# Bias sums ahead of the weights' product, transposed weights copied by ScalarE, u inside the product, and eight row tiles of layer 1 prepared during layer 0

## The chip, the cores and the metric

The kernel runs on one core of a Trainium2 chip. The metric is the device time of one execution in microseconds, as the median of several runs. The four runs of the kernel before agree within 0.32%. Ratios are the mean time of one kernel's runs over that of the other's from the same rounds, so they are not quite the ratio of the medians that stand beside them.

## The reference, cut to what matters

Two layers on 4096 nodes of 512 features. `adj` is a dense 4096 x 4096 matrix of 64 MB that both layers need.

```python
# layer 0: attention inside graphs of 128 nodes, adj as bias
h = relu(layernorm(x))
q = h @ Wq.T + bq;  k = h @ Wk.T + bk;  v = h @ Wv.T + bv
scores = (where(same_graph, q @ k.T * scale, 0) + adj + adj) * where(same_graph, 1, -1e6)
x = x + (softmax(scores) * same_graph) @ v
# layer 1: graph attention, 8 heads of 64
h  = relu(layernorm(x))
mx = einsum('nf,hfd->hnd', h, W)
t  = einsum('hnd,hd->hn', mx, a_dst)
x  = x + softmax(where(adj > 0, s_i + t_j, -inf)) @ mx      # s_i cancels in the softmax
```

## The kernel before

It has four stages. **Start (fold):** the product of Wq and Wk is formed once (`m_sb`), with the terms that the biases give (`c_sb`, `u_sb`, `z_sb`), so that layer 0 needs one projection for q and k together. **Layer 0's loop:** 16 groups `g` of two row tiles of 128 rows. Each group reads two rows of adj ahead (VectorE makes mask bytes, ScalarE sums exponentials, the bytes go out to DRAM), and does scores, values and attention. **Preparation of layer 1:** for each of 32 row tiles, a norm, four transposes, a projection (16 matmul instructions) and a weighting give a tile `part`. **Aggregation:** 3072 matmuls of masks with the parts.

```python
def fold(sb, tmp, work, ps_t, ps_p):
    wkT_sb = load_weight(...); wqT_sb = load_weight(...)
    for n, wT in enumerate((wkT_sb, wqT_sb)):
        ...
        for k in range(KC):                      # KC = 4
            pt = ps_t.tile([P, KC, P], F32, name="pt")        # 3 buffers in PSUM
            for m in range(KC):
                nc.tensor.transpose(pt[:, m, :], wT[:, k, ts(m, P)], ident)
            dst = w[:, :, ts(k, P)]
            if k % 2: nc.vector.tensor_copy(dst, pt)
            else:     nc.scalar.copy(dst, pt)
    for m in range(KC):                          # the product: 32 instructions
        ... matmul(pp, wq[:, k, ts(m, P)], wk[:, k, :]) ...
        nc.scalar.mul(m_sb[:, m, :], pp, SCALE)
    for b in (bk_sb, bq_sb):                     # a bias spread over all rows
        ... matmul(pp[:, ts(k, P)], b[:, k:k+1].to_broadcast([P, P]), ident) ...
    for dst, wT, row in ((u_col, wqT_sb, rows[0]), (c_sb, wkT_sb, rows[1])):
        ... nc.vector.scalar_tensor_tensor(wb, wT[:, k, :], SCALE, row, ..., accum_out=dst[:, k:k+1])
    ...                                          # u_sb and z_sb by matmul and ScalarE copy

for g in range(NG):                              # NG = 16 groups of layer 0
    ...
    s = scores(g, hT, gT, r, *look)
    prepare_on(); prepare_on()                   # only in the last group
    if not last: ngT = queries(nhT)
    sT = turned(s)                               # transposes of s, then a ScalarE copy
    for t in range(G):
        look_on(t)                               # reads adj for the next group
        attend(sT, vs[t], g, t)
        prepare_on()                             # only in the last group
        if not last: nvs.append(values(nhT, t))
    ...
for i in range(len(ahead) - 1, NT):              # the rest of layer 1's row tiles
    nhT = normed1(i + 1)
    prepare(i, hT, part_tile(...))
```

`prepare_on` norms and transposes the next row tile of layer 1 and projects the one before it. The order in the program is a wish, not the order on the chip: when the kernel is compiled, a scheduler moves instructions ahead of others.

## Time and profile before

| | |
|---|---|
| median of 4 runs | 983.44 us (982.24 to 985.37) |
| span of the profiled run | 981.0 us |
| TensorE busy | 947.1 us, 97% |
| mean granted TensorE clock | 0.986 |
| aggregation, not touched by the change | 489.0 us |

TensorE is nearly always busy, so a change of order can win only what it idles and what it loses while its granted clock is below 1 (0.89 on average in the start, 0.94 in the handover). The lines that show where this is stand in the prediction. A line of the timeline gives start, length, engine, source line, operation, and in brackets the idle time of the engine before it with what ended it; a line of the waits gives who waited for whom, the sum in us, the number of times and the longest.

### The profile page before, as it was taken

What the parts mean: (1) busy time and instruction counts of PE and PEld (TensorE: products, weight loads), DVE (VectorE), ACT (ScalarE), POOL (GpSimd) and SP (SyncE); (2) the same over time, 40 slices, a digit from 0 to 9 for tenths busy, and PEclk for the clock granted to TensorE, in tenths of its full rate; (3) what the DMA queues carried; (4) which work ended last, traced back from release to release, by engine and by line L of the source; (5) the groups of instructions that cost most, each with busy time, mean ns of one, the idle gap of its engine ahead of it and who ended that gap; (6) DMA issues with size and microseconds to landing.
All of it is one profiled execution on the core that took longest, in us unless ns stands there. A gap on an engine that the chain in (4) does not pass through costs nothing.

```text
span 981.0 us, 13168 instructions
## 1 busy us (share of the span) xinstructions
PE 947.1 (97%) x5051; PEld 820.8 (84%) x5051; DVE 461.6 (47%) x982; ACT 261.6 (27%) x501; POOL 180.3 (18%) x344
## 2 busy tenths in 40 slices
PE   6899999999999998999999999999999999999995
PEld 4477666766776676888899999999999999999995
DVE  3756866776675287655232423324233242342421
ACT  3676666676671222333100000000000000000000
POOL 1111211221121055555201101011010110101100
PEclk9899999999999998999999999999999999999998
DMA  9949898998992142222013133131221312312111
GB/s 347 419 181 370 352 370 333 377 367 346 368 371 77 59 129 80 65 65 70 6 43 87 50 81 83 47 86 50 80 85 45 86 51 80 86 44 86 50 38 36
DMA packets 58043, 148.28 MB, mean 151 GB/s; under 512 B 6387, under 2 KB 23027, under 8 KB 49779
## 3 DMA queue, kind: packets, MB, share of 16 engines
q1 hardware_dynamic: 48178, 130.31, 38.2%
q10 hardware_dynamic: 9792, 17.05, 4.6%
q8 instruction: 41, 0.67, 0.3%
q14 instruction: 32, 0.25, 0.1%
HBM read 113.77 MB, written 33.55 MB: 150 GB/s over the span
## 4 chain that ended last, share of the span: by engine, by line
PE 86%; DMA 4%; DVE 4%; ACT 3%; POOL 1%; issue 1%; SPq 0%; ACTq 0%; DVEq 0%
PE pg L284 50%; PE pp L418 10%; PE pp L244 9%; PE pp L406 8%; PE pp L491 3%; DMA a<-adj 3%; PE pss L464 2%; PE pt L127 2%; PE pp L190 2%; ACT junk L441 1%; DMA xg<-x 1%; ACT gT L410 1%; POOL part L232 1%; DVE row L121 1%; POOL rstd L120 0%
## 5 line engine op out<-in xcount | busy, mean ns | idle before, releaser
L284 PE MATMUL pg<-part,at 128*128 128x348 f32 x3072 | 489.0, 321 | 1.2 <-DVE e L253 1.2
L284 PEld LDWEIGHTS pg<-part,at 128*128 128x128 f32 x3072 | 488.7, 188 | 1.6 <-issue 1.6
L278 DVE CAST at<-at 128x4096 fp32r<-128x4096 fp8e4 x32 | 73.6, 2301 | 311.6 <-PE pg L284 311.6
L291 ACT COPY tot<-pg 128x522 f32<-128x522 f32 x32 | 19.1, 598 | 469.9 <-PE pg L284 469.9
L441 ACT ACTIVATE junk<-a 128x2048 bf16<-128x2048 f32 (+15 forms) x92 | 124.6, 1355 | 37.4 <-DMA a<-adj 19.4
L244 PE MATMUL pp<-w1x,hT 128*128 128x256 f32 (+1 forms) x512 | 119.5, 387 | 0.0
L418 PE MATMUL pp<-wv,hT 128*128 128x512 f32 x256 | 116.8, 599 | 1.0 <-ACT hT L128 1.0
L406 PE MATMUL pp<-hT,m_sb 128*128 128x256 f32 x512 | 113.2, 379 | 0.0
L244 PEld LDWEIGHTS pp<-w1x,hT 128*128 128x128 f32 x512 | 96.5, 193 | 14.3 <-issue 0.5
L406 PEld LDWEIGHTS pp<-hT,m_sb 128*128 128x128 f32 x512 | 96.1, 190 | 12.9 <-issue 0.5
L418 PEld LDWEIGHTS pp<-wv,hT 128*128 128x128 f32 x256 | 49.1, 193 | 62.0 <-issue 60.4
L136 DVE TENSOR_SCALAR a<-a 128x512 fp8e4<-128x512 f32 x256 | 94.6, 453 | 7.3 <-DMA a<-adj 4.7
L593 POOL COPY den_all<-tot 128x1 f32<-128x1 f32 x31 | 5.8, 186 | 368.2 <-DVE tot L292 368.2
L128 ACT ACTIVATE hT<-pt 128x512 f32<-128x512 f32 x64 | 37.7, 599 | 82.3 <-PE pt L127 82.3
L602 POOL TENSOR_TENSOR tot<-tot,row 128x512 f32<-128x512 f32 x31 | 40.0, 1289 | 62.0 <-DVE tot L297 62.0
L118 POOL TENSOR_SCALAR ve<-mv 128x1 f32<-128x1 f32 x64 | 16.2, 255 | 178.6 <-DVE mv L116 164.8
L232 POOL TENSOR_TENSOR part<-e,part 128x522 fp32r<-128x522 f32 x32 | 42.0, 1312 | 31.4 <-ACT part L231 27.8
L422 DVE TENSOR_TENSOR v<-pp,bv_sb 128x512 f32<-128x512 f32 x32 | 22.1, 691 | 42.3 <-PE pp L418 42.3
L271 DVE STREAM_TRANSPOSE at<-mw 128x1024 f32<-128x1024 f32 x32 | 39.6, 1238 | 0.0
L253 DVE TENSOR_TENSOR e<-pp,e 128x256 f32<-128x256 f32 x64 | 26.7, 418 | 25.3 <-ACT e L372 22.8
L410 ACT ACTIVATE gT<-pp,c_sb 128x256 f32<-128x256 f32 x64 | 29.9, 469 | 31.5 <-PE pp L406 31.4
L120 POOL TENSOR_TENSOR rstd<-ve,neghalf 128x1 f32<-128x1 f32 x64 | 36.8, 578 | 4.6
(94 smaller groups left out, 594.7 us busy)
## 6 DMA issues: line engine op xcount, KB each, us to landing
a<-adj SPq DMA_DIRECT2D x64, 1024.0 KB, 11.9
a_d<-a SPq DMA_DIRECT2D x32, 512.0 KB, 10.2
row<-x_d SPq DMA_DIRECT2D x64, 256.0 KB, 3.4
mw<-a_d SPq DMA_DIRECT2D x128, 128.0 KB, 4.0
xg<-x SPq DMA_DIRECT2D x16, 512.0 KB, 4.6
x_d<-x ACTq DMA_DIRECT2D x32, 256.0 KB, 4.3
out<-tot ACTq DMA_DIRECT2D x31, 256.0 KB, 3.8
wkT_sb<-wkT SPq DMA_DIRECT2D x4, 256.0 KB, 4.6
```

The source lines that it names most:

```text
L128: nc.scalar.activation(dst, pt, AF.Relu)
L136: nc.vector.tensor_scalar(a8v[:, u], av[:, u], 0.0, None, ALU.is_gt, saturate=False)
L232: nc.gpsimd.tensor_sub(dst[:, :, 1, :], e3, dst[:, :, 0, :].bitcast(F32))
L244: nc.tensor.matmul(pm[g][:, :n], hT[:, k, :], w1x[:, k, g * HW : g * HW + n], start=(k == 0), stop=(k == KC - 1),)
L271: nc.vector.transpose(at8.rearrange("p c n b -> p (c n b)").bitcast(F32).rearrange("p (c u n) -> p c u n", c=NW, n=B), mw.rearrange("p u ( ...
L278: nc.vector.tensor_copy(at.rearrange("p (c b) q -> p c b q", b=BY), at8.rearrange("p c q b -> p c b q"))
L284: nc.tensor.matmul(pg[:, c, : 2 * CW1], at[:, j, :], part(j)[:, c].rearrange("p s w -> p (s w)"), start=(j == 0), stop=(j == NT - 1),)
L406: nc.tensor.matmul(pp[:, : G * P], m_sb[:, k, ts(m, P)], hT[:, k, :], start=(k == 0), stop=(k == KC - 1),)
L410: nc.scalar.activation(gT[:, m, :], pp[:, : G * P], AF.Identity, bias=c_sb[:, m : m + 1])
L418: nc.tensor.matmul(pp, hT[:, k, ts(t, P)], wv[:, k, :], start=(k == 0), stop=(k == KC - 1))
L441: nc.scalar.activation(junk[:, c0:c1], a[:, c0:c1], AF.Exp, scale=2.0 * NEG, accum_out=sums[:, n : n + 1],)
L602: nc.gpsimd.tensor_add(num, num, row)
```

## The change

Its intent has two halves. The start is to lose its waits: the bias sums go into the gap in which TensorE waits for weights, all copies of transposed weights (PSUM to SBUF, 128 x 512) go to ScalarE, which takes 587 ns for one in the kernel before where VectorE takes 687 ns, u and z are formed in the middle of the product, and `hu` (each row of h times u, summed) comes after both norms. And eight row tiles of layer 1 are finished during layer 0: one `prepare_on` in every odd group from 3 on, and two more in the last.

```diff
         wkT_sb = load_weight(tmp, wkT, "wkT_sb", KC, tag="lo")
         wqT_sb = load_weight(tmp, wqT, "wqT_sb", KC, tag="lo")
+        def spread_bias(b):
+            pp = ps_p.tile([P, D], F32, name="pp")
+            for k in range(KC):
+                nc.tensor.matmul(
+                    pp[:, ts(k, P)], b[:, k : k + 1].to_broadcast([P, P]), ident,
+                    start=True, stop=True,
+                )
+            row = work.tile([P, D], F32, name="b_row", tag="hn")
+            nc.scalar.copy(row, pp)
+            return row
... (in the loop over the transposed pieces)
-                dst = w[:, :, ts(k, P)]
-                if k % 2:
-                    nc.vector.tensor_copy(dst, pt)
-                else:
-                    nc.scalar.copy(dst, pt)
+                nc.scalar.copy(w[:, :, ts(k, P)], pt)
+                if n == 0 and k == 0:
+                    rows = [spread_bias(b) for b in (bk_sb, bq_sb)]
... (the product and the bias sums are taken out here; the VectorE sums stay, and then)
+        for m in range(KC):
+            if m == 2:
+                ... (u_sb and z_sb, as before but here)
+            ... (the product, as before)
... (in normed)
+                    hns = []
                     for t in range(G):
                         hn = sb.tile([P, D], F32, name="hn")
                         norm(xg[g][:, t, :], hn)
                         relu_T(ps_t, hn, hT[:, :, ts(t, P)])
+                        hns.append(hn)
+                    for t, hn in enumerate(hns):
                         hu = sb.tile([P, D], BF16, name="hu", bufs=1)
... (in the loop over the groups)
-                    if g == 2:
+                    if g == 1:
                         w1x = load_w1(pool1, sb)
...
-                    def prepare_on():
-                        if last:
+                    def prepare_on(now):
+                        if now:
...
                     s = scores(g, hT, gT, r, *look)
-                    prepare_on()
-                    prepare_on()
+                    prepare_on(last)
                     if not last:
                         ngT = queries(nhT)
                     sT = turned(s)
+                    prepare_on(3 <= g and g % 2)
                     nvs = []
                     for t in range(G):
                         look_on(t)
                         attend(sT, vs[t], g, t)
-                        prepare_on()
+                        prepare_on(last and t == 0)
```

More of the change, by code (lines that the diff above doesn't have):

```diff
@@ L186, in fold @@
         z_sb = sb.tile([P, 1], F32, name="z_sb")
-        for m in range(KC):
-            pp = ps_p.tile([P, D], F32, name="pp")
-            for k in range(KC):
-                nc.tensor.matmul(
-                    pp, wq[:, k, ts(m, P)], wk[:, k, :], start=(k == 0), stop=(k == KC - 1)
-                )
-            nc.scalar.mul(m_sb[:, m, :], pp, SCALE)
-        rows = []
-        for n, b in enumerate((bk_sb, bq_sb)):
-            pp = ps_p.tile([P, D], F32, name="pp")
-            for k in range(KC):
-                nc.tensor.matmul(
-                    pp[:, ts(k, P)], b[:, k : k + 1].to_broadcast([P, P]), ident,
-                    start=True, stop=True,
-                )
-            row = work.tile([P, D], F32, name=f"b_row{n}", tag="hn")
-            nc.scalar.copy(row, pp)
-            rows.append(row)
         for dst, wT, row in ((u_col, wqT_sb, rows[0]), (c_sb, wkT_sb, rows[1])):
@@ L215, in fold @@
         )
-        pp = ps_p.tile([P, D], F32, name="pp")
-        for k in range(KC):
-            nc.tensor.matmul(
-                pp[:, ts(k, P)], u_col[:, k : k + 1].to_broadcast([P, P]), ident,
-                start=True, stop=True,
-            )
-        nc.scalar.copy(u_sb, pp)
-        pp = ps_p.tile([P, D], F32, name="pp")
-        nc.tensor.matmul(pp[:, :1], zp.to_broadcast([P, P]), one, start=True, stop=True)
-        nc.scalar.copy(z_sb, pp[:, :1])
+        for m in range(KC):
+            if m == 2:
+                pp = ps_p.tile([P, D], F32, name="pp")
+                for k in range(KC):
+                    nc.tensor.matmul(
+                        pp[:, ts(k, P)], u_col[:, k : k + 1].to_broadcast([P, P]), ident,
+                        start=True, stop=True,
+                    )
+                nc.scalar.copy(u_sb, pp)
+                pp = ps_p.tile([P, D], F32, name="pp")
+                nc.tensor.matmul(pp[:, :1], zp.to_broadcast([P, P]), one, start=True, stop=True)
+                nc.scalar.copy(z_sb, pp[:, :1])
+            pp = ps_p.tile([P, D], F32, name="pp")
+            for k in range(KC):
+                nc.tensor.matmul(
+                    pp, wq[:, k, ts(m, P)], wk[:, k, :], start=(k == 0), stop=(k == KC - 1)
+                )
+            nc.scalar.mul(m_sb[:, m, :], pp, SCALE)
         return m_sb, c_sb, u_sb, z_sb
```

## The prediction

> **What bounds the kernel now.** I read the busy shares of the page first, then the span cut into its stages, then the waits of TensorE stage by stage, then the timeline around each wait. In the busy line, PE is TensorE's matmuls and x is the number of instructions:
>
> ```profile
> PE 947.1 (97%) x5051; PEld 820.8 (84%) x5051; DVE 461.6 (47%) x982; ACT 261.6 (27%) x501; POOL 180.3 (18%) x344
> ```
>
> TensorE is the bound nearly everywhere, and the chain of work that ended last is 86% PE. The change adds and removes no matmul: it only reorders them. So it can gain at most TensorE's 981.0 - 947.1 = 33.9 us of idle time, plus what TensorE loses by running at a lower clock. The busy time by stage says where this is. I chose the borders from the timeline: end of the first `values`, end of the last group's first `scores` (layer 0's main loop), return to a steady pace, first aggregation matmul, last one. Columns: stretch, its length, busy us of each engine, granted clock, DMA share, GB/s:
>
> ```profile
> 0.00:48.38 48.38, 37.11 (x115) 21.16 (x116) 27.09 (x74) 25.50 (x39) 7.67 (x27) 0.89 0.98 382
> 48.38:342.10 293.72, 288.93 (x1227) 199.13 (x1227) 193.36 (x520) 174.29 (x330) 52.21 (x103) 1.00 0.77 299
> 342.10:397.12 55.02, 49.78 (x229) 40.74 (x228) 42.45 (x90) 15.24 (x37) 27.49 (x51) 0.94 0.36 99
> 397.12:480.30 83.18, 81.99 (x414) 70.94 (x412) 44.87 (x104) 26.85 (x63) 46.01 (x100) 1.00 0.21 58
> 480.30:969.33 489.03, 489.00 (x3072) 488.70 (x3072) 150.94 (x185) 19.14 (x32) 46.96 (x63) 1.00 0.23 64
> 969.33:981.00 11.67, 0.30 (x1) 0.08 (x1) 2.93 (x11) 0.60 (x1) 0.00 (x0) 0.58 0.10 32
> ```
>
> The first number after each length is PE. Idle: 11.3 us in the start (at a mean clock of 0.89), 4.8 in layer 0's loop, 5.2 in the handover from layer 0 to layer 1's preparation (at 0.94), 1.2 before the aggregation, nothing in the aggregation, 11.4 in the tail. The last two stages, half of the span, are not touched. What TensorE waited for in the start, in the loop and in the handover (three answers of the waits; us, times, longest):
>
> ```profile
> PE pt L174 <- DMA wkT_sb<-wkT: 5.8, 2, 3.7
> PE pt L174 <- DVE w L177: 2.0, 1, 2.0
> PE pp L218 <- DVE wb L208: 1.3, 3, 0.5
> PE pt L127 <- DVE hn L121: 1.0, 1, 1.0
> PE pp L418 <- ACT hT L128: 1.0, 1, 1.0
> ...
> PE pp L491 <- ACT sT L485: 2.8, 3, 1.3
> PE pt L127 <- DVE hn L121: 1.3, 1, 1.3
> ...
> PE pt L127 <- DVE row L121: 5.2, 4, 3.3
> ```
>
> Of the start's 5.8 us on weight loads, 3.7 is the first load and stays; 2.06 is the wait for the third piece of wkT. Two places of the timeline explain the rest (start, us, engine, line; in brackets the idle time before, and its releaser):
>
> ```profile
> 12.44 1.29 DVE L114 BATCH_NORM_STATS2 stats<-xg 128x6 f32<-128x512 f32 x2 [6.02 <-DMA xg<-x]
> 13.64 1.27 DVE L177 COPY w<-pt 128x512 f32<-128x512 f32 x2
> 14.37 0.66 PE L174 MATMUL pt<-ident,wqT_sb 128*128 128x128 f32 x4 [2.04 <-DVE w L177]
> ...
> 32.01 0.69 DVE L208 SCALAR_TENSOR_TENSOR wb<-wqT_sb,b_row 128x512 bf16<-128x512 f32 x1 [4.06 <-ACT b_row L203]
> ...
> 38.82 2.07 PE L418 MATMUL pp<-wv,hT 128*128 128x512 f32 x2 [0.97 <-ACT hT L128]
> ```
>
> VectorE, queued behind a wait for x, copied the transposed weights late, and TensorE stood 2.04 us for the free PSUM buffer. Then the bias rows came only after the weights' product, so VectorE did the u sums at 32 to 36 us while TensorE had nothing to do.
>
> [...]
> - [...] the product's weight loads are spaced 0.85 us at 15.88 to 18.44 us and 0.43 us from 19.14; the clock of 36 to 40 us is 0.51, of 370 to 375 us 0.56.
> - [...] with only transposes run so far, the four at 14.37 us took 0.66 us, against 1.94 us for the first eight.
> - [...] The trace has 587 and 687 ns, so the new choice of engine costs nothing.
> - [...] TensorE stood 1.32 us at 199.55 us for the sT copy, which ScalarE ran after exponentials that waited for adj.
>
> **The change, part by part.**
>
> *Fold.* Its work on TensorE stays: 32 transposes, 16 bias instructions (1.05 us per eight when warm), 32 product instructions at 0.43 us, 8 for u and 2 for z, 8 transposes of the first h, 16 value instructions at 0.43 us. I rebuild the start. Transposes begin at 3.74 us as now. bk lands by 4.6 us, so the 16 bias instructions fill the 5.7-to-7.75 gap[...] until about 8.5 us. [...] Six groups of four transposes remain; the trace has 0.66 us for a warm group, and ScalarE needs 0.59 us for its copy. The last wqT piece, issued at about 4.65 us with 6.2 us to landing, is there at 10.9, so the last group ends at about 12.5 us. VectorE has both rows and wqT by then, and makes u's four sums (0.7 us each) and c's during the first half of the product (13.8 us): the wait for them disappears. In total: 12.5 + 13.8 (product) + 1.3 (u, z) + 1.3 (first transposes; both norms are done by then, as hu no longer stands between them) + 6.9 (values) = 35.8 us, where the trace has 48.38. I do not take all of that 12.6: [...] ScalarE's exponentials of 1.9 us can delay a copy. I take **10.5 us**, between 8 and 12.5.
>
> *Layer 0's loop.* Before, the last group made four h tiles of layer 1 and finished three tiles; now groups 3, 5, ..., 13 and 15 do this, plus one more in group 15: nine h tiles, eight finished. One tile is 16 product instructions in 3.51 us and four transposes in 0.44 us, so 3.95 us. Five tiles move forward, some 20 us of TensorE, but as it is 98% busy there (288.93 of 293.72), they lengthen the loop by almost what they shorten afterwards. Only the idle 4.8 us can be filled. A group takes 18.7 us now (scores at 113.43 and 132.13) and moves two rows of adj (4.2 MB), their masks (1.0), x (0.5) and x1 (0.5): 6.3 MB, or 336 GB/s, near the 352 to 377 GB/s which the trace shows there. An extra 3.95 us every second group lowers this to 6.4 MB in 20.7 us, 311 GB/s; so the later waits for adj should go. Against this, each inserted tile hangs its transposes on a norm through VectorE, GpSimd, VectorE, which may cost part of a microsecond. Net gain: **1 us**, between -2 and 3. Advancing w1's load from group 2 to 1 moves the 1.3 us wait at 104 us and hardly removes it.
>
> *Handover.* VectorE is 42.45 of 55.02 us busy, with two casts of 2.4 us, three block transposes of 1.2 us and sixteen small comparisons of 0.41 us for the graph check, beside the norms. They stand between a norm and its transposes (3.27 us at 371.39). None of them is removed, and the ring of h tiles still allows one tile ahead, so having eight tiles ready gives TensorE no slack. I take **0.5 us**, between -3 and 5.
>
> Sum: 10.5 + 1 + 0.5 = 12 us; 983.3 - 12 = **971.3 us**.
>
> **Rivals.** (1) *The handover heals.* With more done earlier, VectorE's aggregation set-up may fall where it does not block a norm. Then 5.2 us of idle time and some 2.5 us of lost clock (0.56 and 0.76 over two stretches of 5 us, estimated) would come back: about 964. For it: the title's aim; against it: the work on VectorE there is unchanged. (2) *DMA takes over.* A start 10 us earlier asks for adj earlier, with DMA at 382 GB/s and a share of 0.98 in the first 48 us. Then the gain is given back as waits for sT: about 978 to 982. Against it: in 50 to 75 us the DMA share is 0.46[...]; this reserve moves forward with the start. (3) *New waits for norms* in seven groups, at 1.3 us each as at 104 us: 9 us, about 978. Against it: the row was written groups earlier and queries (6.9 us) cover the norm.
>
> **Range and chances.** The three parts have spreads of about 2, 2 and 3.5 us, together 4.5, so an 80% range of 965 to 978. 2% is 19.7 us, a time below 963.7, which needs nearly all of the best case in every part: 7%. Slower by 2% has no mechanism of that size: 1%.
>
> **What would show it.** Right: values end near 38 us with no wait for wb or L177's copies; clock of the first 50 us over 0.89; loop groups of odd number some 4 us longer; TensorE's idle time in 400 to 480 us as now; the aggregation 489 us. Wrong: a start with waits for ScalarE's copies; new waits of PE on the row norms inside layer 0; sT waits longer than 1.3 us; or a handover without its 5.2 us.

## The result, and the profile after

The median of 4 runs is 971.18 us (969.84 to 972.26), and the ratio 0.9873 (95% interval 0.9851 to 0.9895): 1.3% faster. The predicted time was 971.3.

The page's busy line of the kernel after, and its busy time by stage, with borders at the same events as in the prediction (stretch, length, busy us of each engine with PE first, clock, DMA share, GB/s):

```profile
PE 940.3 (97%) x5051; PEld 817.5 (84%) x5051; DVE 459.4 (47%) x978; ACT 260.7 (27%) x505; POOL 184.0 (19%) x344
...
0.00:37.41 37.41, 31.03 (x115) 17.82 (x116) 21.77 (x63) 24.76 (x39) 11.48 (x25) 1.00 0.96 369
37.41:351.77 314.36, 309.17 (x1327) 217.00 (x1326) 209.54 (x554) 181.41 (x350) 64.71 (x132) 0.99 0.77 301
351.77:405.31 53.54, 47.96 (x228) 39.52 (x227) 41.13 (x89) 14.56 (x36) 26.50 (x50) 0.97 0.32 89
405.31:468.74 63.43, 62.26 (x313) 53.79 (x312) 33.14 (x77) 20.22 (x48) 34.30 (x74) 1.00 0.18 54
468.74:958.40 489.66, 489.62 (x3072) 489.33 (x3072) 150.88 (x185) 19.16 (x33) 46.98 (x63) 1.00 0.23 64
```

The start is 37.41 us long where it was 48.38: the same 115 matmul instructions, at a granted clock of 1.00, with 6.4 us of idle time in place of 11.3. The loop is 20.6 us longer and TensorE is busy for 20.2 us more in it; its idle time is 5.2 us in place of 4.8. The handover idles 5.6 us, 5.2 before. TensorE's busy time fell by 6.8 us although it executes the same 5051 instructions; 6.1 us of this lie in the start (37.11 to 31.03 us for the same 115 instructions), where the mean clock was 0.89 before.

What TensorE waited for in the start, the loop and the handover (waits of the kernel after):

```profile
PE pt L185 <- DMA wkT_sb<-wkT: 3.9, 2, 3.7
PE pt L127 <- DVE hn L121: 1.9, 1, 1.9
PE pp L221 <- ACT m_sb L224: 0.4, 1, 0.4
...
PE pt L127 <- DVE row L121: 2.5, 1, 2.5
PE pp L493 <- ACT sT L487: 2.4, 4, 1.4
...
PE pt L127 <- DVE row L121: 5.6, 4, 3.0
```

And the start on TensorE's timeline:

```profile
3.68 1.09 PE L185 MATMUL pt<-ident,wkT_sb 128*128 128x128 f32 x4 [3.68 <-DMA wkT_sb<-wkT]
4.56 2.00 PE L171 MATMUL pp<-ident,bk_sb 128*128 128x128 f32 x8
6.35 1.21 PE L171 MATMUL pp<-ident,bq_sb 128*128 128x128 f32 x8
...
12.02 7.03 PE L221 MATMUL pp<-w,w 128*128 128x512 f32 x16
...
30.37 0.33 PE L127 MATMUL pt<-ident,hn 128*128 128x128 f32 x1 [1.86 <-DVE hn L121]
```

The bias sums fill the gap that ended at 7.75 us, the product starts at 12.02 us in place of 14.87, and, but for 0.44 us inside the product, nothing stands between its start and the values but one new wait of 1.86 us: the scheduler put a transpose of the next group ahead of the values, and its norm was late.

### The profile page after: what moved, and what is told of

Its sections match the earlier page's. It is cut to its first block, busy times and chain, and to the rows that moved or that the text cites.

```text
span 970.5 us, 13180 instructions
## 1 busy us (share of the span) xinstructions
PE 940.3 (97%) x5051; PEld 817.5 (84%) x5051; DVE 459.4 (47%) x978; ACT 260.7 (27%) x505; POOL 184.0 (19%) x344
## 4 chain that ended last, share of the span: by engine, by line
PE 89%; DVE 3%; DMA 2%; POOL 2%; ACT 2%; issue 1%; SPq 0%; ACTq 0%; DVEq 0%; POOLq 0%
PE pg L283 50%; PE pp L420 11%; PE pp L408 10%; PE pp L243 9%; PE pp L493 3%; PE pss L466 3%; PE pt L127 2%; DMA row<-x_d 1%; POOL part L231 1%; DMA xg<-x 1%; DVE a L136 1%; ACT junk L443 1%; DVE row L121 0%; DVE stats L114 0%; POOL rstd L120 0%
## 5 line engine op out<-in xcount | busy, mean ns | idle before, releaser
L136 DVE TENSOR_SCALAR a<-a 128x512 fp8e4<-128x512 f32 x256 | 98.2, 460 | 0.5 <-DMA a_d<-a 0.4
L118 POOL TENSOR_SCALAR ve<-mv 128x1 f32<-128x1 f32 x64 | 18.7, 295 | 150.9 <-DVE mv L116 150.8
```

Of the source, the lines that this page charges most:

```text
L136: nc.vector.tensor_scalar(a8v[:, u], av[:, u], 0.0, None, ALU.is_gt, saturate=False)
```

## The experiments

Twelve kernels were run, in rounds with the kernel before on the same chip. Their times are medians; spans and stages are from one profiled run each. To compare them, I cut every span at two events: the first matmul of the first group's scores, and that of the last group's scores. "Start" is the time to the first, "loop" the time between the two, "rest" the time after the second. Where tiles move into the loop, 20.2 us of TensorE work moves from rest to loop (five tiles of 3.51 us, six sets of transposes of 0.44 us), so I take it off the loop and add it to the rest in those rows, marked with a star. A tile takes less than that where it is put in: a group without waits is 18.70 us long without a tile and 22.32 with one, so 3.62 us for 3.95 us of work. Five tiles thus fill 1.7 us of gaps too short to be listed as waits, and the starred loops contain this gain.

| kernel | median us | ratio to before (95%) | span | start | loop | rest |
|---|---|---|---|---|---|---|
| before | 983.44 | 1 | 981.0 | 55.99 | 283.99 | 641.0 |
| full change * | 971.18 | 0.9873 (0.9851 to 0.9895) | 970.5 | 45.08 | 284.7 | 640.7 |
| e1 new start alone | 979.1 | 0.9959 (0.993 to 0.9989) | 973.9 | 44.21 | 288.0 | 641.7 |
| e2 tiles alone * | 979.72 | 0.9956 (0.9934 to 0.9978) | 977.8 | 55.36 | 282.3 | 640.2 |
| e3 bias first alone | 983.05 | 0.9991 (0.997 to 1.0012) | 980.0 | 50.60 | 288.8 | 640.6 |
| e4 ScalarE copies alone | 979.57 | 0.9957 (0.9934 to 0.998) | 977.4 | 53.48 | 283.8 | 640.1 |
| e6 full, u late * | 970.36 | 0.9863 (0.9846 to 0.988) | 967.8 | 43.05 | 285.0 | 639.8 |
| e7 full, graph check early * | 968.94 | 0.9852 (0.9837 to 0.9867) | 965.4 | 45.03 | 284.8 | 635.6 |
| e9 e7 and cut set-up * | 968.85 | 0.9856 (0.9834 to 0.9879) | 967.1 | 44.86 | 283.7 | 638.5 |
| e10 e1, fewer bytes | 982.99 | 0.9984 (0.9964 to 1.0004) | 978.4 | 44.80 | 291.7 | 641.9 |
| e11 e1, exponentials behind sT | 986.05 | 1.0038 (1.0017 to 1.0058) | 982.2 | 44.98 | 298.8 | 638.4 |
| e12 full, exponentials behind sT * | 974.3 | 0.9916 (0.9887 to 0.9944) | 973.8 | 44.22 | 291.6 | 638.0 |
| e13 e7, set-up held back * | 964.64 | 0.9821 (0.9802 to 0.984) | 961.8 | 44.49 | 283.0 | 634.3 |
| e15 e13, e12 and rows earlier * | 968.53 | 0.9865 (0.9842 to 0.9888) | 964.9 | 44.28 | 288.3 | 632.3 |

The start column alone shows that the first half of the change shortens the start in every kernel that has it. The other two columns decide what is left of that.

### e1, e2: the two halves of the change, each alone

e1 is the changed kernel with the preparation put back:

```diff
-                    if g == 1:
+                    if g == 2:
                         w1x = load_w1(pool1, sb)
...
                     prepare_on(last)
+                    prepare_on(last)
...
-                    prepare_on(3 <= g and g % 2)
...
-                        prepare_on(last and t == 0)
+                        prepare_on(last)
```

> Only the start is changed (bias sums first, ScalarE copies, u inside the product, hu after both norms); layer 1's tiles are prepared where the kernel before prepares them, and w1 is loaded in group 2. My theory, that the whole gain is made in the first 50 us: 972 us (971 to 974), that is as fast as the full change, with the first queries at about 37.4 us. Rival, that the eight prepared tiles give a part of it: 975 us or more.

Measured: 979.1 us (975.73 to 985.83). The rival holds: only 4 us of the 12 come from the new start alone. The first queries did start at 36.54 us, and the start is 11.8 us shorter than before; but in the profiled run, which is the fastest of the six, the loop lost 4.0 us again. Its waits, in the loop, and the largest of them on the timeline:

```profile
PE pp L493 <- ACT sT L487: 8.3, 8, 3.1
...
245.37 1.91 ACT L443 ACTIVATE junk<-a 128x2048 bf16<-128x2048 f32 x1 [2.42 <-DMA a<-adj]
...
247.64 0.36 ACT L487 COPY sT<-pss 128x256 f32<-128x256 f32 x1
248.05 1.13 PE L493 MATMUL pp<-v,sT 128*128 128x512 f32 x2 [3.08 <-ACT sT L487]
```

ScalarE waited 2.42 us for a half row of adj, summed its exponentials for 1.91 us, and only then copied sT, for which TensorE stood 3.08 us. This is the prediction's second rival (the gain is given back as waits for sT, "about 978 to 982"): it does come true, but only where the tiles are not moved.

e2 is the kernel before with only the tiles moved.

> Only the eight tiles move into layer 0 (and w1's load to group 1); the start is that of the kernel before. My theory, that this moves TensorE's work from one stage where it is the bound to another: 983 us (981 to 986), each inserted group some 4 us longer and the later stage shorter by as much, TensorE idle 5 us in the handover as before. Rival, that the handover or the waits for adj heal: 979 us or less.

Measured: 979.72 us, 4.0 us better than the before of its rounds (983.72), between my theory and the rival. The profiled run shows 3.2 us: 0.6 in the start, 1.7 in the loop, 0.9 in the rest. The handover did not heal: 5.6 us of waits for row norms, 5.2 before. The waits for sT in the loop are 4.0 us, where before had 2.8 and another of 1.3; so the loop's 1.7 us is not explained by its waits: it is the 1.7 us of gaps that five tiles fill (above). In the start, the product ran at full clock in this run (the clock of 16 to 20 us is 1.00, 0.63 before), without any change there.

The two halves together give 12.3 us and alone 4.6 and 4.0 (medians against the before of the same rounds). **They come out worth more together than apart, by some 4 us:** the product of their ratios is 0.9915, and the full change has 0.9873. Taken as independent, the three intervals leave about 4 us either way on this difference (my estimate from the table), so it stands at the edge of the noise; the full change but for u (e6, below) has 0.9863.

### e3, e4: the start taken apart

e3 moves only the bias sums, e4 only the copies:

```diff
+                if n == 0 and k == 0:
+                    rows = [spread_bias(b) for b in (bk_sb, bq_sb)]     # e3
...
-                if k % 2:
-                    nc.vector.tensor_copy(dst, pt)
-                else:
-                    nc.scalar.copy(dst, pt)
+                nc.scalar.copy(w[:, :, ts(k, P)], pt)                   # e4
```

> The kernel before with only the bias sums moved ahead, to the gap after the first transposes; copies still alternate between the engines, u still comes after the product. My theory: the 2.06 us wait for the third piece of wkT is filled by work that is taken out later, and VectorE's sums no longer stand between product and values, with the clock no longer falling there: 6 to 9 us faster, 974.5 to 977.5 us; the 2 us wait of the last transposes for VectorE's copy stays. Rival, that the order of u and of hu in the queues matters more: less than 4 us, above 979 us.

Measured: 983.05 us, no gain; the rival's number, for a reason that neither named. The start is 5.4 us shorter, and the loop gives 4.8 of it back, with 9.2 us of waits for sT, much as in e1. And a wait in the start has grown (timeline of e3):

```profile
12.02 1.29 DVE L114 BATCH_NORM_STATS2 stats<-xg 128x6 f32<-128x512 f32 x2 [7.25 <-DMA xg<-x]
...
14.77 1.28 DVE L188 COPY w<-pt 128x512 f32<-128x512 f32 x2
15.51 2.82 PE L185 MATMUL pt<-ident,wqT_sb 128*128 128x128 f32 x12 [5.20 <-DVE w L188]
```

With the bias sums early, VectorE has two more sums ready ahead of its copies, and all of it is queued behind the statistics of x, which wait for their transfer until 12.02 us. TensorE stood 5.20 us where it stood 2.04 before, and the product started at 18.13 us.

> The kernel before with only the copies of the transposed weights all on ScalarE. My theory: the 2.04 us wait before the last four transposes goes, the product starts 2 us earlier, nothing else moves: 981.4 us (980.5 to 982.5). Rival, that ScalarE falls behind with eight copies of 0.59 us: no gain, 983 us or more.

Measured: 979.57 us (978.22 to 981.94), 4.2 us better than the before of its rounds: better than expected. The wait of 2.04 us is gone and the product starts at 11.76 us, 3.1 earlier. Only transposes had run on TensorE by then. The product's weight loads are spaced by 0.43 us from 12.19 us on, and the clock of 12 to 20 us is 1.00, where before those from 15.88 to 18.44 us were 0.85 us apart and the clock of 16 to 20 us was 0.63. In the profiled run, 2.5 us of the 3.6 lie in the start.

So alone the copies gain 4 us and the early bias sums nothing, but the start does not explain this: e3 shortens it by 5.4 us and e4 only by 2.5. The loop does. Without moved tiles, the two kernels with a start of 44 to 51 us wait 8.3 and 9.2 us for sT in the loop (e1, e3), those with one of 53 to 56 us only 2.6 and 2.8 (e4, before). Which part of the new start the full change needs was not run, except for u:

### e6: u behind the product

```diff
-            if m == 2:
-                ...                              # u_sb, z_sb between the halves of the product
...
             nc.scalar.mul(m_sb[:, m, :], pp, SCALE)
+        ...                                      # the same lines, after the product
```

> The full change, but u and z are formed after the product, as in the kernel before. Theory, that with the bias sums early the place of u no longer matters to TensorE (10 short instructions, 1.3 us, on either side): 971 us, within 1.5 us of the full change. Rival, that u's copy and hu, coming 7 us later, hold up VectorE's queue and with it the first groups: 974 us or more.

Measured: 970.36 us (969.61 to 971.06), as the theory has it. "u inside the product" is not part of the gain; with u late the start is even 2 us shorter in the profiled run (43.05 us).

### e10, e11, e12: why the loop takes the start's gain back

The waits of e1 have two causes that can be told apart in principle: too many bytes for the shorter groups, or an unlucky order in ScalarE's queue. e10 takes bytes away from e1 (wrong result):

```diff
-                        if h:
+                        if h and i % 2 == 0:
                             nc.sync.dma_start(a_d[i], a8.bitcast(F32))
...
-            tot = aggregate(sb3, ps_g, i, lambda j: parts[j])
+            tot = aggregate(sb3, ps_g, i - i % 2, lambda j: parts[j])
```

> The kernel with the new start alone (979.1 us), but the mask bytes of odd row tiles are not written out, and the aggregation reads those of the even tile twice: wrong result on purpose. A group then moves 5.8 MB in place of 6.3 MB, as little per us as with the eight inserted tiles. Theory, that the adj stream takes back what the new start gains, and that the inserted tiles help by stretching the groups: the waits of TensorE for sT fall from 8.4 to under 4 us and the time to 971 to 974 us. Rival, that the order in ScalarE's queue makes these waits whatever DMA does: 977 us or more, the waits as before.

Measured: 982.99 us; the rival's number. The waits for sT did not fall (9.7 us in the loop). But the experiment is not clean: the compiled order changed with the transfers. Counted from the two kernels' instructions, ScalarE now had up to three half rows of exponentials (6016 columns) between the scores' exponentials and sT, where e1 has at most two (3968). So it shows that fewer bytes alone do not help, not that bytes play no part.

e11 and e12 leave the bytes and change the order, in e1 and in the full change. `issue_after` only settles the place in ScalarE's queue; no wait is taken away:

```diff
-                                nc.scalar.activation(
-                                    junk[:, c0:c1], a[:, c0:c1], AF.Exp, ...)
+                                with ExitStack() as order:
+                                    if behind is not None and (i % G or h):
+                                        order.enter_context(tc.issue_after(behind.ins))   # sT's copy
+                                    nc.scalar.activation(
+                                        junk[:, c0:c1], a[:, c0:c1], AF.Exp, ...)
```

> The new start alone (979.1 us), with one thing added: in each group of layer 0, ScalarE issues all the exponentials of adj but those of the first half row behind the copy of sT. Nothing is removed and no byte fewer is moved. Theory, that ScalarE's queue turns a late adj half row into a wait of TensorE, because exponentials stand ahead of sT: waits for sT under 2 us in layer 0's loop (8.4 before), 972 us (970.5 to 974.5), as fast as with the eight inserted tiles. Rival, that the adj stream itself is too slow for the shorter groups: the wait moves to the scores or to the next group, 977 us or more.

Measured: 986.05 us, slower than the kernel before. The theory falls. The waits of e11's loop:

```profile
PE pt L127 <- DVE hn L121: 10.7, 14, 2.8
PE pp L496 <- ACT sT L490: 2.4, 4, 0.6
PE pp L408 <- ACT hT L128: 1.6, 1, 1.6
```

The waits for sT did go (2.4 us, 8.3 in e1), but norms took their place. The timeline shows how: the exponentials are the last use of an adj buffer, so later exponentials free the seven buffers later and the next loads can start only later (e11's DMA share from 150 to 200 us is 0.83, e1's 0.91), and VectorE, whose queue has mask bytes ahead of the norms, waits for adj (a wait of 3.73 us for adj stands before the mask bytes at 184.44 us, and TensorE's wait of 2.66 us for a norm at 191.88). **In these runs the order on ScalarE chose where the late adj half row was felt, not whether it was late.** That the buffers are the link is read from the trace; no run shows it alone.

> The full change with the same order on ScalarE. Theory: its four waits for sT (2.4 us) go, the others stay, 969 us (967.5 to 970.5). Rival, that the exponentials, started later, fall behind and hold up the next group's scores: 971 us or more.

Measured: 974.3 us (970.69 to 978.3), 3 us slower than the full change: the rival. The loop is 6.9 us longer in the profiled run.

What follows for e1: with the start 11 us earlier TensorE asks for each adj row earlier, and the stream of buffer, load, read, free does not follow. An inserted tile gives this stream 3.62 us more in every second group, and the waits for sT fall from 8.3 us to 2.4. A rival is that a tile, which stands between the transposes of s and the product that needs sT, only hides a late sT. It does not explain most of the fall: 5.6 us of e1's waits stand in groups 6, 10 and 12, which have no tile, and they are gone in the full change. That the longer groups let the stream follow is thus argued from the traces; no clean run shows it. Whether the stream is slow through its bytes or through the turn-around of its seven buffers is not settled; e1's DMA share of 0.91 to 0.95 from 45 to 250 us would allow either.

### e7, e9, e13: the handover

The full change leaves 5.6 us of waits for row norms after the loop. The longest on its timeline (kernel after):

```profile
373.12 2.26 DVE L277 CAST at<-at 128x4096 fp32r<-128x4096 fp8e4 x1
373.41 3.07 POOL L231 TENSOR_TENSOR part<-e,part 128x522 fp32r<-128x522 f32 x1 [4.16 <-ACT e L371]
...
377.57 1.23 POOL L231 TENSOR_TENSOR part<-e,part 128x522 fp32r<-128x522 f32 x1
377.64 1.44 DVE L121 TENSOR_SCALAR row<-row,mv,rstd 128x512 f32<-128x512 f32 x1 [0.94 <-POOL rstd L120]
...
379.14 1.12 PE L127 MATMUL pt<-ident,row 128*128 128x128 f32 x4 [3.02 <-DVE row L121]
```

VectorE casts mask bytes for the aggregation's second tile in the midst of the preparation. The scheduler had placed this there. While the cast runs, GpSimd's `part` takes 3.07 us in place of 1.23, the small norm steps on GpSimd come behind it, and the norm itself takes 1.44 us in place of 0.55 beside the next `part`. e7 moves the graph check to group 4 of layer 0, where VectorE has room (in the kernel after it is busy for 36.25 of the 50 us from 100 to 150 us):

```diff
+                    if g == 4:
+                        graphs_are_tiles(sb)
... (cut: a memset of `held` moves to the top, `cmp` shares another tile's buffer)
-                graphs_are_tiles(sb3)
```

> The full change with the graph check (some 25 small VectorE instructions, 7.5 us) moved from the handover to group 4 of layer 0. Theory, that the handover's 5.6 us of idle TensorE come from the aggregation's block transposes and casts standing between norm and transposes: the 3.0 us wait stays, the small waits at 389 and 397 us (2.1 us) go; 969 us (968 to 970.5). Rival, that the small comparisons are the cause: all of the waits go, and with them the half clock: 965 us or less.

Measured: 968.94 us (967.27 to 970.58), the theory's number. The waits for row norms after 350 us fall to 2.3 us; the wait behind the cast stays, at 1.9 us. The rest is 5.1 us shorter, more than the 3.3 us of waits; the clock of 345 to 400 us is 1.00.

e9 also cuts the block transposes and the casts of the first two aggregation tiles into four pieces each, with `for q in range(4)` around them.

> As the previous one, and the block transposes and casts of the first two aggregation tiles cut in four pieces each (0.3 and 0.6 us), so that a norm can pass between them. Theory: TensorE's waits for row norms in the handover fall from 5.6 us to under 2, the clock stays up there, 965.5 us (963.5 to 967.5). Rival, that the work as such is too much for VectorE and GpSimd, cut or not: as the previous one, 969 us or more.

Measured: 968.85 us; the theory fails and the rival's number holds. A wait of 3.14 us for a row norm is still there, because the scheduler put three of the pieces one behind the other (timeline of e9):

```profile
375.89 2.95 DVE L283 CAST at<-at 128x1024 fp32r<-128x1024 fp8e4 x3
...
383.41 1.09 PE L128 MATMUL pt<-ident,row 128*128 128x128 f32 x4 [3.14 <-DVE row L122]
```

e13 settles the place instead: in e7, VectorE's set-up for aggregation tiles 0 and 1 is queued behind the norms of row tiles 24 and 31.

```diff
+        with ExitStack() as order:
+            if isinstance(i, int) and i < 2:
+                order.enter_context(tc.issue_after(norms[(24, 31)[i]].ins))
             nc.vector.transpose(...)
             nc.vector.tensor_copy(...)
```

> The full change with the graph check in layer 0 and VectorE's block transposes and casts for the first two aggregation tiles held behind the norm of row tile 24 and that of tile 31. Theory, that these are what stands between norm and transposes in the handover: the waits for row norms after 350 us fall from 5.6 (full change) or 2.3 us (graph check moved) to under 1.5 us, the clock stays full, 967 us (965.5 to 968.5). Rival, that they cost the same wherever they stand among the norms: 968.9 us or more, as with the graph check alone.

Measured: 964.64 us (963.66 to 965.63), ratio 0.9821: better than expected, and the fastest of all kernels here. Its wait for row norms after 348 us, and the stretch of 345 to 400 us in busy time by engine:

```profile
PE pt L128 <- DVE row L122: 1.5, 1, 1.5
...
345.00:400.00 55.00, 55.00 (x274) 46.10 (x273) 28.82 (x70) 16.79 (x41) 25.53 (x56) 1.00 0.22 68
```

TensorE is busy for all of the 55 us at a clock of 1.00. So the handover's loss was VectorE's foreign work among the norms: taken out of it, its wait is gone, and one of 1.5 us remains, at 427 us. From the full change to e13 the rest falls from 640.7 to 634.3 us. But not all of e13's lead over e7 is this: of the 3.6 us between their profiled runs only 1.3 lie in the rest, and 1.8 lie in the loop, where both wait 2.5 us for the same row norm in group 8. After it, the products with sT and the values of one row tile took 1.91 and 4.00 us in e7, 1.02 and 3.60 us in e13: the clock of 200 to 250 us is 0.97 in e7 and 1.00 in e13. Why it fell after the one wait and not after the other is not shown.

### e15: all together

e13 with the order of e12, and each row of layer 1 loaded one tile earlier.

> The full change with all of it: graph check in layer 0, aggregation set-up held back, exponentials behind sT, and each layer 1 row loaded one tile earlier (which should take away the 2.5 us wait at 217 us, where the row's transfer was queued for 10 us behind adj loads). Theory, that the gains add up: 971.2 - 4 (handover) - 2 (sT) - 2.5 (row) = 963 us (961.5 to 966). Rival, that one wait takes the place of another: 967 us or more.

Measured: 968.53 us (966.5 to 972.86), 4 us slower than e13: the rival. The earlier rows do what they should (no wait for a row norm is left in the loop), and the rest is the shortest of all, but the order on ScalarE costs more than that, as in e12: the loop is 5.3 us longer than e13's. The sum without that order was not run.

## Why the prediction was right, point by point

**The time** of 971.18 us lies 0.1 us from the predicted 971.3. The mechanism of the start was right in its parts; what keeps its gain was not seen. The agreement to 0.1 us is luck: between the profiled runs the difference is 10.5 us (start 10.9, loop a loss of 0.7, rest 0.3), while the medians differ by 12.3.

- **Start, "I take 10.5 us":** measured 11.0 us (values end at 37.41 us, 48.38 before); the rebuilt sum said 35.8 without a margin. The bias sums ended by 7.6 us, earlier than the estimated 8.5, since the second eight took 1.21 us where the first eight had taken 2.00; the product began at 12.02 us (12.5 predicted); the margin went into a wait for a norm (1.86 us) and one for `m_sb` (0.44 us), and the mean clock of the start was 1.00. The waits for wb and for L177's copies are gone, as said.
- **Loop, "Net gain: 1 us":** measured a loss of 0.4 to 0.7 us, by which border is taken, inside the given range. "The later waits for adj should go" was right for most groups after 150 us and wrong before: four waits for sT of 2.4 us in all remain, up to 132 us. And in group 8 the next tile waits 2.48 us for its norm, since its row's transfer, issued at 203.66 us, took 10.7 us to land; this looks like the third rival, in one group of seven. But the timeline of the kernel after shows a late adj under it:

```profile
213.82 1.91 ACT L443 ACTIVATE junk<-a 128x2048 bf16<-128x2048 f32 x1 [1.68 <-DMA a<-adj]
216.09 0.36 ACT L487 COPY sT<-pss 128x256 f32<-128x256 f32 x1
216.93 0.44 PE L127 MATMUL pt<-ident,row 128*128 128x128 f32 x2 [2.48 <-DVE row L121]
...
218.06 5.29 PE L420 MATMUL pp<-wv,hT 128*128 128x512 f32 x8
```

  sT was copied only at 216.09 us, so without the norm TensorE would have stood there some 2 us for sT (estimated from these lines), and the norm alone cost about 0.5. The eight value instructions after it took 5.29 us in place of 3.60 (the clock of 218 to 224 us is 0.72), and the group took 22.98 us in place of 18.70, the largest loss in the loop. The prediction's estimate for the loop had no such loss of clock. In the prediction's text, "plus one more in group 15" should be two more; its count of nine h tiles is right.
- **Handover, "I take 0.5 us":** the rest is 0.3 us shorter. The waits are 5.6 us, 5.2 before, and the clock a little better (0.97 against 0.94). "None of them is removed" was the right reason; e7 and e13 show it by removing them.
- **Where the reasoning was wrong:** I took the three terms as independent and gave the tiles 1 us. The new start alone gains 4.0 to 4.6 us, not 10.5, for the loop takes back the rest, as the second rival said; I had argued this rival away with the DMA reserve of 50 to 75 us (a share of 0.46). With the tiles most of the start's gain is kept: from e1 to the full change the median falls by 7.9 us (3.4 us between the profiled runs, of which e1's is its fastest). So the term "Loop" was mis-sized as a worth of the tiles, and right only as a difference between before and after.
- **What the title names:** "u inside the product" is worth nothing (e6), and the early bias sums, though they shorten the start by 5.4 us, gain nothing by themselves (e3).

## What to carry to other kernels

Two changes that look independent need not add up: here the loop took back much of what a shorter start had gained (e1, e3), and less of it when work was moved into the loop. Before adding up terms, ask whether the stream that the next stage waits for can follow. When an engine idles at a border of stages, look for work of a later stage that the scheduler has put there early, and settle its place by an order (e13); cutting it into pieces did not settle it here (e9). A wait that is moved off one queue by an order can come back on another (e11, e12). Here an order alone, with the same instructions, moved the kernel by some tenths of a per cent: from e7 to e13 the ratio to before falls from 0.9852 to 0.9821 (part of it is the clock in group 8), from e1 to e11 it rises from 0.9959 to 1.0038.
